# A latent-attention and ternary-GLU kernel: order of the first block's transfers, roots, transposes and queries

## The chip, the cores and the metric

The kernel runs on one core of a Trainium2 chip, in one launch. The metric is the device time of that core in microseconds (us). A core has TensorE (PE, with its weight loads PEld), VectorE (DVE), ScalarE (ACT), GpSimd (POOL) and SyncE (SP), which here does nothing but issue transfers. Each engine takes its own instructions in order. Times inside a profile are counted from the start of its span.

## The reference

The input is x, 4096 rows of 512 (two sequences of 2048). A normalised copy of x goes through an attention over 64 fixed latent keys for each of 16 heads, in which only the four largest logits of a row and head are kept; the result is normalised and added to x. Then a gated expert layer follows whose three weights are reduced to the signs -1, 0, 1 times one scale for each matrix; its result is normalised and added as well.

```python
Q = (hidden_states @ Wq.T + bq)...
V = (hidden_states @ Wv.T + bv)...
attn_logits = einsum('bhtd,lhd->bhtl', Q, latent) / sqrt(HD)
topk_logits, topk_idx = top_k(attn_logits, 4)
attn_weights = softmax(topk_logits)
weighted = einsum('bhtk,bhtkd->bhtd', attn_weights, selected)
return (weighted + V)... @ Wo.T + bo
...
scale = mean(abs(w)) + EPS                  # ternary_quant, for wu, wg and wd
q = clip(round(w / scale), -1, 1) * scale
...
hidden = silu(x @ wu.T) * (x @ wg.T)
return hidden @ wd.T
...
x = x + layernorm(attention(layernorm(x)))
x = x + layernorm(ffn(layernorm(x)))
```

The three scales need the sum of absolute values of the whole of a matrix. So no sign of a weight can be formed before that matrix has been read and summed.

## The kernel before

**Tiling.** The 4096 rows are worked in eight blocks of 512 rows, each of four tiles of 128 rows. The 2048 expert columns are 16 chunks of 128. For a block, an expert loop runs over the 16 chunks: the `u` product (8 matmuls: four slices of the 512 inputs, each with a high and a low half of the input), the `g` product likewise, the gate on ACT and DVE, and the `down` product of the chunk before it. Between these instructions stand the pieces of the next block's attention, so PE has both to do.

**The first stretch.** Block 0 has no expert loop to hide its attention. Its instructions, the reading and summing of the expert weights and the first part of block 1's attention are put in an order written out by hand, the string `FIRST_STEPS`. Each word is a step with its tile, head pair or piece: the table `STEPS` says what it calls, and nothing is reordered later. Words that the change touches:

- `ast`, `ars`, `aap`, `atr`, `acp`: block 0's first normalisation. Statistics of a tile on DVE (L245, L246), its root on POOL (`rstd`, L252 and L253), the normalised row on DVE (L272), its transposition on PE into a PSUM bank (`transpose_row`, L282) and the copy to SBUF (ACT, and DVE for tile 2; L591, L589). Before, `ars` works on two tiles at a time.
- `q`, `qc`: a query chunk on PE (L597) and its copy with the bias on ACT (L604). `bh`, `bl`: bias of the output, which reads bo. `l`, `lc`: logits of two head pairs and their copy on ACT (L622). `m`, `r`, `e`, `n`: the four largest, their replacement, the exponentials, the weights. `v`, `t`, `tc`, `y`, `yc`, `o`: values, transposed weights, their product, output.
- `su`, `sg`, `sd` with a piece number: sum of absolute values of one piece of raw weights on ACT (L202). u and g have eight pieces of 512 KB, d has six of 512 KB and four of 256 KB. `totu`, `totg`, `totd`: the sums over partitions on PE (L210). `scu`, `scg`, `scd`: the scales on DVE. `rd`: rounding on POOL (L226); signs follow on ACT (L233). `scd` also makes the scale of the output (L843 to L847).
- `nst`, `nap`, `ntr`, `ncp`, `nq`, `nqc`: the same normalisation and the four queries of block 1. `nq1`, `nq2`, `nq3` stand behind the first block's last outputs.
- `ost`, `onm`, `oap`, `oad`: the output's normalisation. `fst`, `frs`, `fap`, `ftr`, `fhi`, `flo`: the normalisation ahead of the experts. Statistics, root, row, transposition on PE, the high half on ACT (L701), the low half on DVE (L707). Then block 0's expert loop begins (L724 for `u` and `g`, L767 for `down`).

**PSUM.** There are eight banks: two for `at_psum` (used in turn by logits, transposes, block 1's queries and totals), one each for `u` and `g`, four for `acc_psum` (block 0's queries, then its four output tiles, then the expert accumulators). In a turn, a bank is taken again when its last reader is done.

**Transfers.** All go through SP's queue in the order of the program: block 0's four x tiles, wq, lk (the latent keys), bqv (biases), wv, lv, bo, block 1's x, the u pieces 0 to 7, g 0 to 7, wo, d 0 to 9. Each word of `FIRST_STEPS` that reads one of them waits for its landing. SP issues a transfer only when an earlier one, some eight before it, has landed.

**Order around the change.** At the start: x, statistics, roots, rows, transposes, copies, then the first query. At the end: block 1's queries 1, 2, 3 on PE, then the four transposes in the two banks of `at_psum`, the total of d in the same banks, and the first expert product.

Of the kernel before, what the change touches and what calls it, by code (L numbers as in the profile page):

```python
# [17 lines left out]
P = 128  # L18
# [14 lines left out]


FIRST_STEPS = """
ast0 ast1 ast2 ars0 ast3 aap0 ars1 aap1 atr0 aap3 atr1 acp0 aap2 atr3 acp1 atr2 acp3 acp2 q0 bh
q1 qc0 bl nst0 l0 nst3 qc1 su0 nst1 v0 lc0 nst2 lc1 nrs su2 m1 su3 m0 l1 su1 r0 q2 lc2 su5 nap0
e0 r1 su6 ntr0 qc2 q3 ncp0 nap3 su7 nap1 nap2 sg1 n0 sg2 ob0 ob1 m2 ob2 e1 v1 qc3 n1 lc3 sg4 r2
sg5 t0 t1 tc0 ob3 tc1 m3 ntr2 e2 ntr1 ncp2 r3 y0 ncp1 l2 yc0 sg7 o3_0 n2 e3 o2_0 sd0 n3 v3 lc5
lc4 m5 sd2 m4 sd3 t3 r4 t2 su4 o0_0 tc2 o1_0 tc3 r5 sd6 y1 sd7 l3 yc1 e4 o1_1 lc7 n4 e5 o0_1 lc6  # L40
o2_1 n5 sd9 totu sd8 t4 o3_1 tc4 scu sg6 m6 rdu2 t5 v2 tc5 r6 rdu4 sgu2 rdu6 sgu4 m7 rdu0 sgu6
ntr3 y2 ncp3 r7 sgu0 nq0 yc2 e6 e7 n6 sg0 o0_2 n7 nqc0 sd1 t6 o2_2 tc6 t7 sg3 o1_2 tc7 totg sd5
y3 scg rdg6 o3_2 yc3 rdg4 o2_3 sgg6 o3_3 ost2 rdg0 sgg4 o1_3 ost3 ors2 sgg0 o0_3 ost1 ors3 nq1
sd4 onm2 ost0 ors1 oap2 onm3 oap3 ors0 oad2 oad3 rdg2 onm0 fst2 oap0 nq2 nqc1 oad0 frs2 sgg2
onm1 fst3 oap1 fap2 frs3 oad1 fst1 nq3 nqc2 fap3 frs1 fst0 fap1 frs0 ftr3 fap0 nqc3 fhi3 ftr0
flo3 fhi0 flo0 ftr1 fhi1 ftr2 flo1 fhi2 flo2 totd scd rdd0 rdd1
"""

LAST_O = ((0, 3), (1, 3), (2, 3), (3, 3))
# [9 lines left out]
def latent_attention_ternary_glu(  # L59
# [15 lines left out]
    nc = tc.nc  # L75
    NT, D = x_in.shape
    E = wuT.shape[1]
    DC = D // P
# [18 lines left out]
    def at_psum(name):  # L97
        return ps_at.tile([P, 512], F32, tag="at", name=name)
# [11 lines left out]
    def transposed(which, b, name, dtype):  # L110
        return work.tile([P, DC, TB], dtype, tag=f"{which}{b % 2}", name=name, bufs=1)
# [8 lines left out]
    halves = [(k, h) for k in range(DC) for h in range(2)]  # L120
    raw = {}
# [5 lines left out]
    count = {"u": 2 * DC, "g": 2 * DC, "d": 2 * DC + 2}  # L127

    def load_x(b):
        x_tiles[b] = []  # L130
        for t in range(TT):
            xt = work.tile([P, D], F32, tag="x", name=f"x_{b}_{t}", bufs=2 * TT)
            r = b * TB + t * P
            nc.sync.dma_start(out=xt, in_=x_in[r : r + P, :])
            x_tiles[b].append(xt)
# [7 lines left out]
            out=normed[b], in_=x_in[b * TB : (b + 1) * TB, :].rearrange("(t p) d -> p t d", p=P)  # L143
        )

    def load_up(n, src):
        for i, (k, h) in enumerate(halves):
            nc.sync.dma_start(
                out=raw[n, i], in_=src[k * P : (k + 1) * P, h * CH : (h + 1) * CH]
            )  # L150

    load_x(0)
    wq = wpool.tile([P, DC, D], F32, name="wq")
    wv = wpool.tile([P, DC, D], F32, name="wv")
    wo = wpool.tile([P, DC, D], F32, name="wo")
    bqv_sb = wpool.tile([P, 2, DC], F32, name="bqv_sb")
    bo_sb = wpool.tile([P, D], F32, name="bo_sb")
    lk = wpool.tile([P, DC, 2 * L], F32, name="lk")
    lv = wpool.tile([P, H // 2, HP], F32, name="lv")
    nc.sync.dma_start(out=wq, in_=wqT.rearrange("(c p) n -> p c n", p=P))  # L160
    nc.sync.dma_start(out=lk, in_=latk)
    nc.sync.dma_start(out=bqv_sb, in_=bqv)
    nc.sync.dma_start(out=wv, in_=wvT.rearrange("(c p) n -> p c n", p=P))
    nc.sync.dma_start(out=lv, in_=latv)
    nc.sync.dma_start(out=bo_sb, in_=bo.to_broadcast([P, D]))
    load_x(1)
    load_up("u", wuT)
    load_up("g", wgT)
    nc.sync.dma_start(out=wo, in_=woT.rearrange("(c p) n -> p c n", p=P))
    for i in range(count["d"]):  # L170
        rows = 2 * P if i < 6 else P
        r = i * 2 * P if i < 6 else 12 * P + (i - 6) * P
        nc.sync.dma_start(
            out=raw["d", i].rearrange("p (c n) -> p c n", n=D),
            in_=wdT[r : r + rows, :].rearrange("(c p) n -> p c n", p=P),
        )


    both = work.tile([P, 2, P], F32, tag="hid", name="ones", bufs=2)
# [14 lines left out]
    tern = {}  # L194
# [5 lines left out]
    def sum_abs(n, i):  # L200
        w = raw[n, i]
        nc.scalar.activation(  # L202
            junk[:, : w.shape[-1]], w, AF.Abs, accum_out=sums[n][:, i : i + 1]
        )

    totals = {}

    def total(n):
        totals[n] = at_psum(f"tot_{n}")
        nc.tensor.matmul(  # L210
            totals[n][:, : count[n]], lhsT=ones, rhs=sums[n], start=True, stop=True
        )

    def scale(n):
        total = small.tile([P, 1], F32, tag="wtotal", name=f"total_{n}", bufs=1)
        nc.vector.tensor_reduce(total, totals[n][:, : count[n]], AX.X, ALU.add)
        sc = columns[:, 1 + "ugd".index(n) : 2 + "ugd".index(n)]
        nc.vector.tensor_scalar(sc, total, 1.0 / (D * E), QUANT_EPS, ALU.mult, ALU.add)
        scales[n] = sc
        inv = columns[:, 4 + "ugd".index(n) : 5 + "ugd".index(n)]  # L220
        nc.vector.reciprocal(inv, sc)
        inverses[n] = inv
# [53 lines left out]
    def row(name):  # L276
        return work.tile([P, D], F32, tag="row", name=name, bufs=4)

    def transpose_row(h, name):
        pt = at_psum(f"pt_{name}")  # L280
        for c in range(DC):
            nc.tensor.transpose(pt[:, c * P : (c + 1) * P], h[:, c * P : (c + 1) * P], ident)  # L282
        return pt.rearrange("p (c k) -> p c k", k=P)
# [288 lines left out]
    class FirstAttention(SecondAttention):  # L572
# [12 lines left out]

        def a_copy(self, t):
            dst, src = self.hT[:, :, t * P : (t + 1) * P], self.pt.pop(t)
            if self.b == 0 and t == 2:
                nc.vector.tensor_copy(dst, src)  # L589
            else:  # L590
                nc.scalar.copy(dst, src)  # L591

        def q_pe(self, c, psum):
            self.pq = getattr(self, "pq", {})
            self.pq[c] = psum(f"pq_{self.b}_{c}")
            for k in range(DC):
                nc.tensor.matmul(  # L597
                    self.pq[c], lhsT=wq[:, k, c * P : (c + 1) * P], rhs=self.hT[:, k, :],
                    start=(k == 0), stop=(k == DC - 1),
                )  # L600

        def q_copy(self, c, qT):
            self.qT[c] = qT
            nc.scalar.activation(qT, self.pq.pop(c), AF.Identity, bias=bqv_sb[:, 0, c : c + 1])  # L604
# [88 lines left out]
            nc.vector.tensor_tensor(x_tiles[self.b][t], x_tiles[self.b][t], self.rows.pop(("o", t)), ALU.add)  # L693

        def f_trans_pe(self, t):
            self.pt[t] = transpose_row(self.rows.pop(("f", t)), f"f{self.b}_{t}")

        def f_high(self, t):
            if not hasattr(self, "hi"):
# [13 lines left out]
    class Experts:  # L713
# [5 lines left out]

        def up(self, n, e):  # L720
            p = ps_up.tile([P, TB], F32, tag=n, name=f"p{n}_{self.b}_{e}")
            for k in range(DC):
                for i, part in enumerate(self.parts):
                    nc.tensor.matmul(  # L724
                        p, lhsT=tern[n, 2 * k + e // 8][:, (e % 8) * P : (e % 8 + 1) * P], rhs=part[:, k],
                        start=(k == 0 and i == 0), stop=(k == DC - 1 and i == 1),
                    )
            (self.pu if n == "u" else self.pg)[e] = p


# [97 lines left out]
    A = FirstAttention(0)  # L828
    nxt = FirstAttention(1)
# [6 lines left out]
        half_u.append(half)  # L836

    def scale_out():
        scale("d")

        first = columns[:, 8:9]
        square = columns[:, 9:10]
        nc.vector.tensor_scalar(first, half_u[0], scales["g"], scales["d"], ALU.mult, ALU.mult)  # L843
        nc.vector.tensor_tensor(square, first, first, ALU.mult)
        least = columns[:, 10:11]
        nc.vector.reciprocal(least, square)
        nc.vector.tensor_scalar(least, least, LN_EPS, 0.0, ALU.mult, ALU.add)  # L847
        out_scale.extend((first, square, least))


    def query_place(c):
        if c < 3:
            if not hasattr(nxt, "early"):
                nxt.early = transposed("Y", 1, "qT_1", F32)
            return nxt.early[:, c, :]
        return work.tile([P, TB], F32, tag="qT", name=f"qT_1_{c}", bufs=1)


    def first_query_place(c):
        tag = ("hid_hi", "hid_lo")[c // 2]  # L860
        return work.tile([P, TB], F32, tag=tag, name=f"qT_0_{c}", bufs=2)

    STEPS = {
        "ast": A.a_stats,
        "ars": lambda j: A.a_rstd(2 * j, 2 * j + 2),
        "aap": A.a_apply,
        "atr": A.a_trans_pe,
        "acp": A.a_copy,
# [1 line left out]
        "qc": lambda c: A.q_copy(c, first_query_place(c)),  # L870
        "l": A.l_pe,
        "lc": A.l_copy,
        "m": A.m,
        "r": A.r,
        "e": A.e,
# [24 lines left out]
        "ntr": nxt.a_trans_pe,  # L900
        "ncp": nxt.a_copy,
        "nq": lambda c: nxt.q_pe(c, at_psum),
        "nqc": lambda c: nxt.q_copy(c, query_place(c)),
        "totu": lambda: total("u"),
        "totg": lambda: total("g"),
        "totd": lambda: total("d"),
        "scu": half_scale,
        "scg": lambda: scale("g"),
        "scd": scale_out,
    }  # L910
    for n in "ugd":
        STEPS["s" + n] = lambda i, n=n: sum_abs(n, i)
        STEPS["rd" + n] = lambda i, n=n: rounded(n, i)
        STEPS["sg" + n] = lambda i, n=n: sign(n, i)
    for step in FIRST_STEPS.split():
        name, numbers = re.fullmatch(r"([a-z]+)([0-9_]*)", step).groups()
        STEPS[name](*(int(v) for v in numbers.split("_") if v))

# [143 lines left out]
    for b in range(NB):  # L1062
        if b > 0:
            A, nxt = nxt, after
# [141 lines left out]
```

## Time and profile before

| what | us |
|---|---|
| median of three runs (lowest, highest) | 1152.59 (1152.09, 1153.02) |
| the profiled execution | 1154.03 |
| its span | 1152.1 |
| PE, DVE, ACT, POOL busy in the span | 1134.6, 841.5, 402.6, 167.6 |
| first query matmul starts | 12.44 |
| last weight piece's stretch of full DMA traffic ends | about 51 |
| first expert matmul starts | 90.59 |
| mean granted TensorE clock | 0.997 |

The profile is of one execution. An engine's share is an average over the whole span; what a change in one stretch is worth has to be read in that stretch, in the timelines (start, duration, engine, source line, what was written from what, how often, and in brackets the idle time before with what ended it) and in tables of windows. A busy PE is a modelled figure: matmuls are pipelined, so the distance between the starts of two of them says more than the duration of one.

```profile
PEclk9999999999999999999999999999999999999999
DMA  9700211023111322133222222232321412102001
GB/s 346 302 0 1 73 56 55 1 68 116 65 46 37 111 91 74 54 102 101 85 80 73 74 95 98 65 91 75 108 76 55 110 65 93 62 1 74 37 1 37
```

These are lines of the page's 40 slices of 28.8 us: the clock granted (in tenths, 9 is 0.9 or more), the share of the 16 DMA engines and what they moved. The weights come in the first two slices.

### The profile page before, as it was taken

The numbers are of one execution on the slowest core, as the hardware profiler recorded it, in microseconds if no ns is written. First come the engines' busy times: TensorE is split into PE (matmuls) and PEld (weight loads), VectorE is DVE, ScalarE is ACT, GpSimd is POOL, SyncE is SP. The second block draws the span as 40 slices with busy tenths as digits, with TensorE's granted clock in tenths as the row PEclk, the third lists the DMA queues.
The fourth block names the chain that finished last, engine by engine and source line by source line (L and its number), as shares of the span: only waits on it lengthen the run. The fifth ranks groups of instructions, "written<-read, shape, count | busy, mean of one in ns | idle before, by whom it ended". The sixth has DMA issues, their size and how long they took to land.

```text
span 1152.1 us, 14493 instructions
## 1 busy us (share of the span) xinstructions
PE 1134.6 (98%) x4650; PEld 776.8 (67%) x4650; DVE 841.5 (73%) x2939; ACT 402.6 (35%) x701; POOL 167.6 (15%) x203
## 2 busy tenths in 40 slices
PE   8999999999999999999999999999999999999997
PEld 5547665876757676676657766586675766768785
DVE  6976984968866978668876788677886787847435
ACT  4985531332313332333314333143322433224223
POOL 1056001310022100320003200022001120030100
PEclk9999999999999999999999999999999999999999
DMA  9700211023111322133222222232321412102001
GB/s 346 302 0 1 73 56 55 1 68 116 65 46 37 111 91 74 54 102 101 85 80 73 74 95 98 65 91 75 108 76 55 110 65 93 62 1 74 37 1 37
DMA packets 89355, 90.87 MB, mean 79 GB/s; under 512 B 7872, under 2 KB 62400, under 8 KB 89280
## 3 DMA queue, kind: packets, MB, share of 16 engines
q1 hardware_dynamic: 89280, 89.95, 24.5%
q8 instruction: 37, 0.61, 0.2%
q14 instruction: 38, 0.31, 0.1%
HBM read 56.37 MB, written 33.55 MB: 78 GB/s over the span
## 4 chain that ended last, share of the span: by engine, by line
PE 88%; DVE 5%; DMA 3%; ACT 2%; SPq 1%; issue 0%; POOL 0%; DVEq 0%; ACTq 0%
PE pg L724 20%; PE acc L767 19%; PE pu L724 19%; PE po L464 8%; PE pv L436 8%; PE pq L349 7%; PE pv L453 2%; PE pl L363 2%; DMA raw_d<-in_wdT 1%; DMA raw_g<-in_wgT 1%; PE pq L597 1%; DMA bo_sb<-in_bo 1%; DVE left L389 1%; DMA raw_u<-in_wuT 1%; ACT junk L202 1%; PE pt_f L282 0%
## 5 line engine op out<-in xcount | busy, mean ns | idle before, releaser
L724 PE MATMUL pg<-hT_f,tern_g 128*128 128x512 f32 x512 | 208.3, 407 | 0.0
L724 PE MATMUL pu<-hT_f,tern_u 128*128 128x512 f32 x512 | 205.5, 401 | 0.0
L767 PE MATMUL acc<-tern_d,hi 128*128 128x512 f32 x512 | 203.5, 398 | 0.0
L767 PE MATMUL acc<-tern_d,lo 128*128 128x512 f32 x512 | 200.0, 391 | 2.3 <-DVE lo L757 2.1
L724 PE MATMUL pu<-lT_f,tern_u 128*128 128x512 f32 x512 | 200.4, 391 | 0.1
L724 PE MATMUL pg<-lT_f,tern_g 128*128 128x512 f32 x512 | 199.6, 390 | 0.0
L733 ACT ACTIVATE h<-pu,columns 128x512 f32<-128x512 f32 x128 | 87.1, 681 | 203.0 <-PE pu L724 202.7
L752 ACT CAST hi<-h 128x512 fp32r<-128x512 f32 x128 | 79.2, 619 | 216.8 <-DVE h L741 216.8
L736 DVE SCALAR_TENSOR_TENSOR h<-h,pu 128x512 f32<-128x512 f32 x128 | 86.0, 672 | 86.6 <-ACT h L733 86.6
L741 DVE TENSOR_TENSOR h<-h,pg 128x512 f32<-128x512 f32 x128 | 86.4, 675 | 66.4 <-PE pg L724 65.3
L767 PEld LDWEIGHTS acc<-tern_d,hi 128*128 128x128 f32 x512 | 96.1, 188 | 32.8 <-issue 13.4
L724 PEld LDWEIGHTS pg<-hT_f,tern_g 128*128 128x128 f32 x512 | 96.3, 188 | 25.4 <-issue 1.7
L767 PEld LDWEIGHTS acc<-tern_d,lo 128*128 128x128 f32 x512 | 96.1, 188 | 24.4 <-DVE lo L757 3.9
L724 PEld LDWEIGHTS pu<-hT_f,tern_u 128*128 128x128 f32 x512 | 96.5, 188 | 23.9 <-issue 2.4
L724 PEld LDWEIGHTS pu<-lT_f,tern_u 128*128 128x128 f32 x512 | 96.6, 189 | 23.0 <-issue 2.9
L724 PEld LDWEIGHTS pg<-lT_f,tern_g 128*128 128x128 f32 x512 | 96.3, 188 | 22.2 <-issue 3.4
L757 DVE TENSOR_TENSOR lo<-h,hi 128x512 fp32r<-128x512 f32 x128 | 92.5, 723 | 25.4 <-ACT hi L752 25.4
L436 PE MATMUL pv<-hT,wv 128*128 128x512 f32 x224 | 100.7, 592 | 0.2 <-ACT w L371 0.2
L389 DVE MATCH_REPLACE8 left<-m,w 128x64 f32<-128x64 f32 x512 | 100.3, 209 | 0.0
L464 PE MATMUL po<-wo,attnT 128*128 128x512 f32 x224 | 97.3, 592 | 0.0
L349 PE MATMUL pq<-hT,wq 128*128 128x512 f32 x192 | 86.6, 594 | 0.3 <-PE acc L767 0.3
L464 PEld LDWEIGHTS po<-wo,attnT 128*128 128x128 f32 x224 | 42.5, 190 | 50.8 <-issue 48.6
(144 smaller groups left out, 1317.4 us busy)
## 6 DMA issues: line engine op xcount, KB each, us to landing
dz<-z SPq DMA_DIRECT2D x56, 256.0 KB, 2.0
wT<-dz SPq DMA_DIRECT2D x224, 64.0 KB, 1.9
x<-in_x SPq DMA_DIRECT2D x32, 256.0 KB, 3.9
out_x<-x SPq DMA_DIRECT2D x31, 256.0 KB, 2.0
xa<-in_x SPq DMA_DIRECT2D x6, 1024.0 KB, 5.3
far_a<-za SPq DMA_DIRECT2D x20, 256.0 KB, 3.0
hT<-far_a SPq DMA_DIRECT2D x20, 256.0 KB, 5.3
far_f<-zf SPq DMA_DIRECT2D x20, 256.0 KB, 2.8
```

The source lines that it names most:

```text
L349: nc.tensor.matmul(pq, lhsT=wq[:, k, c * P : (c + 1) * P], rhs=self.taken(k), start=(k == 0), stop=(k == DC - 1),)
L363: nc.tensor.matmul(pls[pr][:, t * P : (t + 1) * P], lhsT=qT[rows, t * P : (t + 1) * P], rhs=lk[rows, c, :], start=True, stop=True, tile_po ...
L389: nc.vector.match_replace(left[:, g, :], m8[:, g, :], w[:, g, :], TAKEN)
L436: nc.tensor.matmul(self.pv[c], lhsT=wv[:, k, c * P : (c + 1) * P], rhs=self.ordered(k), start=(k == 0), stop=False,)
L464: nc.tensor.matmul(self.po[t], lhsT=self.attnT[:, c, t * P : (t + 1) * P], rhs=wo[:, c, :], start=(c == 0), stop=(c == DC - 1),)
L724: nc.tensor.matmul(p, lhsT=tern[n, 2 * k + e // 8][:, (e % 8) * P : (e % 8 + 1) * P], rhs=part[:, k], start=(k == 0 and i == 0), stop=(k = ...
L733: nc.scalar.activation(self.h[e], self.pu[e], AF.Tanh, scale=half_u[0])
L736: nc.vector.scalar_tensor_tensor(self.h[e], self.h[e], 1.0, self.pu.pop(e), ALU.add, ALU.mult)
L741: nc.vector.tensor_tensor(self.h[e], self.h[e], self.pg.pop(e), ALU.mult)
L752: nc.scalar.copy(hi, self.h[e])
L757: nc.vector.tensor_tensor(lo, self.h.pop(e), self.hid[e][0].bitcast(F32), ALU.subtract)
L767: nc.tensor.matmul(self.acc[t], lhsT=part[:, t * P : (t + 1) * P], rhs=wd, start=(e == 0 and i == 0), stop=(e == EC - 1 and i == 1),)
```

## The change

1. **`hold`.** A new step behind the first tile's statistics clears one column of the lk tile on DVE and then issues every transfer that stood behind wq. lk's transfer writes the same place, so it waits for that clearing, and SP's queue stands behind it.
2. **Order of transfers.** The pieces of u, g and d are issued in another order, with wo between the fourth and the fifth piece of g.
3. **Roots tile by tile.** `ars` takes a range of tiles: 0 and 1, then 2, then 3. The rows, transposes and copies run in the order 0, 1, 2, 3, and tile 3's copy is the one on DVE.
4. **Block 1's last query in parts.** `nq3` becomes four pieces of two passes each (`nqp3_0` to `nqp3_3`), put between the transposes `ftr2`, `ftr3`, `ftr1`, `ftr0`; its copy `nqc3` comes behind the high halves.
5. **Banks.** Transposes of tiles 0 and 1, the parts of the query and the total of d use `acc_psum`.
6. **Total and scale.** `totd` stands ahead of the transposes. `scd` makes the scale of d alone, before the last low halves; the scale of the output becomes its own step `sco` behind them.
7. **First expert.** In block 0's first `u` product, the four matmuls of the high half come first, then those of the low half. One further step, `sg5`, stands five words later.

```diff
-ast0 ast1 ast2 ars0 ast3 aap0 ars1 aap1 atr0 aap3 atr1 acp0 aap2 atr3 acp1 atr2 acp3 acp2 q0 bh
+ast0 hold ast1 ars0_2 ast2 ars2_3 ast3 ars3_4 aap0 aap1 atr0 aap2 atr1 acp0 aap3 atr2 acp1 atr3 acp2 acp3 q0 bh
...
-onm1 fst3 oap1 fap2 frs3 oad1 fst1 nq3 nqc2 fap3 frs1 fst0 fap1 frs0 ftr3 fap0 nqc3 fhi3 ftr0
-flo3 fhi0 flo0 ftr1 fhi1 ftr2 flo1 fhi2 flo2 totd scd rdd0 rdd1
+onm1 fst3 oap1 fap2 frs3 oad1 totd fst1 ftr2 nqc2 fhi2 nqp3_0 fap3 frs1 fst0 ftr3 nqp3_1 fhi3 fap1
+frs0 flo2 ftr1 nqp3_2 fhi1 fap0 ftr0 nqp3_3 fhi0 scd flo3 flo1 flo0 sco nqc3 rdd0 rdd1
...
+    def load_weights():
+        nc.sync.dma_start(out=lk, in_=latk)
...
+        load_x(1)
+        load_up("u", wuT, (0, 2, 3, 1, 5, 6, 7, 4))
+        load_up("g", wgT, (1, 2, 4, 5))
+        nc.sync.dma_start(out=wo, in_=woT.rearrange("(c p) n -> p c n", p=P))
+        load_up("g", wgT, (7, 6, 0, 3))
+        for i in (0, 2, 3, 6, 7, 9, 8, 1, 5, 4):
...
     def total(n):
-        totals[n] = at_psum(f"tot_{n}")
+        totals[n] = (acc_psum if n == "d" else at_psum)(f"tot_{n}")
...
-            if self.b == 0 and t == 2:
+            if self.b == 0 and t == 3:
                 nc.vector.tensor_copy(dst, src)
...
+        def q_part(self, c, k, psum):
+            if k == 0:
+                self.pq[c] = psum(f"pq_{self.b}_{c}")
+            nc.tensor.matmul(
+                self.pq[c], lhsT=wq[:, k, c * P : (c + 1) * P], rhs=self.hT[:, k, :],
+                start=(k == 0), stop=(k == DC - 1),
+            )
...
         def f_trans_pe(self, t):
-            self.pt[t] = transpose_row(self.rows.pop(("f", t)), f"f{self.b}_{t}")
+            psum = at_psum if t in (2, 3) else acc_psum
+            self.pt[t] = transpose_row(self.rows.pop(("f", t)), f"f{self.b}_{t}", psum)
...
+            pairs = [(k, i) for k in range(DC) for i in range(2)]
+            if self.b == 0 and e == 0 and n == "u":
+
+                pairs.sort(key=lambda pair: pair[1])
...
     def scale_out():
-        scale("d")
...
+    def hold_weights():
+        nc.vector.memset(lk[:, 0, 0:1], 0.0)
+        load_weights()
...
-        "ars": lambda j: A.a_rstd(2 * j, 2 * j + 2),
+        "ars": A.a_rstd,
...
+        "nqp": lambda c, k: nxt.q_part(c, k, acc_psum),
...
-        "scd": scale_out,
+        "scd": lambda: scale("d"),
+        "sco": scale_out,
```

More of the change, by code (lines that the diff above doesn't have):

```diff
@@ L35 @@
 FIRST_STEPS = """
-ast0 ast1 ast2 ars0 ast3 aap0 ars1 aap1 atr0 aap3 atr1 acp0 aap2 atr3 acp1 atr2 acp3 acp2 q0 bh
+ast0 hold ast1 ars0_2 ast2 ars2_3 ast3 ars3_4 aap0 aap1 atr0 aap2 atr1 acp0 aap3 atr2 acp1 atr3 acp2 acp3 q0 bh
 q1 qc0 bl nst0 l0 nst3 qc1 su0 nst1 v0 lc0 nst2 lc1 nrs su2 m1 su3 m0 l1 su1 r0 q2 lc2 su5 nap0
 e0 r1 su6 ntr0 qc2 q3 ncp0 nap3 su7 nap1 nap2 sg1 n0 sg2 ob0 ob1 m2 ob2 e1 v1 qc3 n1 lc3 sg4 r2
-sg5 t0 t1 tc0 ob3 tc1 m3 ntr2 e2 ntr1 ncp2 r3 y0 ncp1 l2 yc0 sg7 o3_0 n2 e3 o2_0 sd0 n3 v3 lc5
+t0 t1 tc0 ob3 tc1 sg5 m3 ntr2 e2 ntr1 ncp2 r3 y0 ncp1 l2 yc0 sg7 o3_0 n2 e3 o2_0 sd0 n3 v3 lc5
 lc4 m5 sd2 m4 sd3 t3 r4 t2 su4 o0_0 tc2 o1_0 tc3 r5 sd6 y1 sd7 l3 yc1 e4 o1_1 lc7 n4 e5 o0_1 lc6
@@ L144, in load_normed, with load_up @@
         )
-    def load_up(n, src):
-        for i, (k, h) in enumerate(halves):
+    def load_up(n, src, pieces):
+        for i in pieces:
+            k, h = halves[i]
             nc.sync.dma_start(
@@ L160, in latent_attention_ternary_glu @@
     nc.sync.dma_start(out=wq, in_=wqT.rearrange("(c p) n -> p c n", p=P))
[L161 to L176, printed above, removed]
+    def load_weights():
+        nc.sync.dma_start(out=lk, in_=latk)
+        nc.sync.dma_start(out=bqv_sb, in_=bqv)
+        nc.sync.dma_start(out=wv, in_=wvT.rearrange("(c p) n -> p c n", p=P))
+        nc.sync.dma_start(out=lv, in_=latv)
+        nc.sync.dma_start(out=bo_sb, in_=bo.to_broadcast([P, D]))
+        load_x(1)
[4 more added lines that the diff above has]
+        for i in (0, 2, 3, 6, 7, 9, 8, 1, 5, 4):
+            rows = 2 * P if i < 6 else P
+            r = i * 2 * P if i < 6 else 12 * P + (i - 6) * P
+            nc.sync.dma_start(
+                out=raw["d", i].rearrange("p (c n) -> p c n", n=D),
+                in_=wdT[r : r + rows, :].rearrange("(c p) n -> p c n", p=P),
+            )
     both = work.tile([P, 2, P], F32, tag="hid", name="ones", bufs=2)
@@ L277, in row, with transpose_row @@
         return work.tile([P, D], F32, tag="row", name=name, bufs=4)
-    def transpose_row(h, name):
-        pt = at_psum(f"pt_{name}")
+    def transpose_row(h, name, psum=at_psum):
+        pt = psum(f"pt_{name}")
         for c in range(DC):
@@ L600, in q_pe @@
                 )
+        def q_part(self, c, k, psum):
[4 more added lines that the diff above has]
+                start=(k == 0), stop=(k == DC - 1),
+            )
         def q_copy(self, c, qT):
@@ L721, in up @@
             p = ps_up.tile([P, TB], F32, tag=n, name=f"p{n}_{self.b}_{e}")
[L722 to L727, printed above, removed]
+            pairs = [(k, i) for k in range(DC) for i in range(2)]
+            if self.b == 0 and e == 0 and n == "u":
+                pairs.sort(key=lambda pair: pair[1])
+            for k, i in pairs:
+                nc.tensor.matmul(
+                    p, lhsT=tern[n, 2 * k + e // 8][:, (e % 8) * P : (e % 8 + 1) * P],
+                    rhs=self.parts[i][:, k], start=(k, i) == pairs[0], stop=(k, i) == pairs[-1],
+                )
             (self.pu if n == "u" else self.pg)[e] = p
@@ L872, in latent_attention_ternary_glu @@
         "lc": A.l_copy,
+        "hold": hold_weights,
         "m": A.m,
```

## The prediction

> **What bounds the kernel now.** I read the busy shares first, then ten- and two-microsecond windows to find where TensorE is not full, then the engines' timelines there. Times are from the span's start.
>
> ```profile
> PE 1134.6 (98%) x4650; PEld 776.8 (67%) x4650; DVE 841.5 (73%) x2939; ACT 402.6 (35%) x701; POOL 167.6 (15%) x203
> ...
> 84.00:86.00 2.00, 2.00 (x6) 0.90 (x5) 1.25 (x4) 0.00 (x0) 1.51 (x4) 1.00 0.01 4
> 86.00:88.00 2.00, 1.40 (x9) 0.78 (x7) 0.94 (x2) 1.38 (x3) 0.00 (x0) 1.00 0.00 0
> 88.00:90.00 2.00, 1.31 (x8) 0.84 (x8) 1.33 (x3) 1.11 (x3) 0.00 (x0) 1.00 0.00 0
> 90.00:92.00 2.00, 1.52 (x5) 1.10 (x6) 1.73 (x7) 0.43 (x1) 0.28 (x1) 0.85 0.00 0
> 92.00:94.00 2.00, 2.00 (x6) 1.53 (x5) 1.16 (x3) 0.00 (x0) 2.00 (x3) 0.50 0.06 12
> ```
>
> The first line is the page's; the others are windows (columns: length, PE, PEld, DVE, ACT and POOL busy, granted clock, DMA share, GB/s). TensorE bounds the whole, so a gain must be time that PE waits or runs slowly. Such time lies here in two places: the start, and 86 to 95, where PE idles and is then granted half its clock.
>
> ```profile
> 75.85 10.46 PE L597 MATMUL pq<-hT,wq 128*128 128x512 f32 x24
> 86.15 0.60 PE L282 MATMUL pt_f<-ident,h_f 128*128 128x128 f32 x4
> 87.09 0.66 PE L282 MATMUL pt_f<-ident,h_f 128*128 128x128 f32 x4 [0.34 <-ACT qT L604]
> 88.29 0.66 PE L282 MATMUL pt_f<-ident,h_f 128*128 128x128 f32 x4 [0.55 <-DVE lT_f L707]
> 89.15 0.66 PE L282 MATMUL pt_f<-ident,h_f 128*128 128x128 f32 x4 [0.20 <-DVE lT_f L707]
> 90.35 0.39 PE L210 MATMUL tot_d<-sums_d,ones 128*128 128x10 f32 x2 [0.55 <-DVE lT_f L707]
> 90.59 0.48 PE L724 MATMUL pu<-hT_f,tern_u 128*128 128x512 f32 x1
> 91.21 0.66 PE L724 MATMUL pu<-lT_f,tern_u 128*128 128x512 f32 x1
> ```
>
> PE's timeline (start, duration, idle before and releaser): the second block's last three queries, then four row transposes that wait for two PSUM banks to be emptied by ACT and DVE, then the sum for the down weights, then the experts.
>
> ```profile
> 5.68 0.69 DVE L245 BATCH_NORM_STATS2 st_a<-x 128x6 f32<-128x512 f32 x1 [0.28 <-DMA x<-in_x]
> 7.44 0.69 DVE L245 BATCH_NORM_STATS2 st_a<-x 128x6 f32<-128x512 f32 x1 [0.84 <-DMA x<-in_x]
> 9.83 1.00 DVE L272 TENSOR_SCALAR h_a<-x,mv_a,rs_a 128x512 f32<-128x512 f32 x2 [0.59 <-POOL rs_a L253]
> 12.44 7.10 PE L597 MATMUL pq<-hT,wq 128*128 128x512 f32 x16 [0.83 <-ACT ones L660]
> 22.31 1.11 DVE L381 MAX8 m<-w 128x8 f32<-128x64 f32 x8 [0.90 <-ACT w L622]
> 43.27 1.06 ACT L202 ACTIVATE junk<-raw_d 128x1024 bf16<-128x1024 f32 x1 [0.33 <-DMA raw_d<-in_wdT]
> 46.20 1.06 ACT L202 ACTIVATE junk<-raw_d 128x1024 bf16<-128x1024 f32 x1 [0.80 <-DMA raw_d<-in_wdT]
> 53.12 0.19 DVE L404 TENSOR_REDUCE ri<-top 128x8 f32<-128x32 f32 x1 [0.49 <-ACT top L398]
> ```
>
> These are lines of the DVE, PE and ACT timelines up to 70. From 12.44 three engines are nearly full together (ten-microsecond windows give DVE 88 to 96%, ACT 85 to 97% between 20 and 50), and DMA moves about 400 GB/s until 51. ACT waits for raw_d at 43.27 and 46.20, so an earlier start is worth only what the transfers let through.
>
> **Part 1, the start.** After the first tile's statistics DVE now clears one column of lk (0.1 us, as its other small memsets at 0.09), and lk's transfer, with all behind it on SP's queue, waits for that. lk was issued at 3.05; now after the statistics end (4.44), about 4.6: 1.55 later. Behind it stand bqv, wv, lv, bo, the second block's x and all expert weights. Ahead are x and wq, 2.1 MB, of which the windows up to 4.5 have moved about 0.8; at the 400 GB/s seen later the rest lasts beyond 7.7. The first x was issued at 0.72 and its bytes show between 1.5 and 2.0, so lk's would flow at about 5.9. The engines stay fed: I cost the hold at 0 for the stream, bounded by +1.55 (the whole delay) and -2.0 (2 to 8.5 us moved about 270 GB/s; at 390 the same bytes need 2.0 less).
>
> The last x tile lands at 7.4, and wq's early bytes compete with it anyway; I take 0.4 for it (0 to 1.8, if it followed the third by no more time than its statistics). Roots tile by tile take away the 0.59 wait at 9.83. So q0 starts about 1.0 earlier (0.6 to 2.4). POOL issues six small operations rather than four (0.19 and about 0.6 each), beside DVE's work.
>
> What comes through? DVE's first max (22.31) waits for ACT, but its own statistics of the second block end at 21.41, after the bias row that needs bo (15.55, same place in the stream): at most 0.85 of gain there. At 43.27 ACT sums raw_d 0. Ahead of it in the new order are the same bytes (all u and g, wo), so it still lands at 43.25, and the two logit copies behind it on ACT release DVE's next max at 44.9 instead of 45.25: only 0.35 is left. But raw_d 1 now comes after 2 and 3, each of which lands 0.5 MiB, 1.36 us, earlier (ten such transfers follow at 1.35 to 1.45). ACT then runs 43.27 + 1.1 + 1.05 (copies) + two sums of 1.18 + raw_u 4 at 1.18, ending at about 48.8 against 49.9: 1.1 earlier. DVE, 0.35 earlier, no longer waits 0.49 at 53.12 nor 0.1 behind it: 0.9 to 1.0. From there DVE and ACT hand on to each other to PE's sum at 69.97. **I take 1.0**, bounds -0.55 (1.0 less 1.55) and +2.0. wo four transfers earlier removes PE's 0.34 wait at 41.97, inside the same 1.0.
>
> **Part 2, queries between transposes.** From 75.85 PE has: 24 query matmuls, 10.30 to the next start; four rows of transposes at 0.53 each (61.05 to 61.58 elsewhere in the timeline); the sum at 0.32. Together 12.74, so the experts could begin at 88.59 instead of 90.59: **2.0**. For this every transpose must find its row and bank. With nothing else moved, PE asks for row 2 at 83.0, row 3 at 84.4, row 1 at 85.8, row 0 at 87.2 (two queries to 82.7, then the sum, and after each transpose a piece of 0.86). Rows are normalised at 81.64, 83.98, 85.24 and 86.49 by DVE's timeline: slack 1.4, 0.4, 0.6, 0.7. Banks: rows 2 and 3 use those of queries 1 and 2, whose copies end by 80.2 and 83.6; the sum, the query and rows 1 and 0 use the four output banks, the last of which is read at 81.88. The extra low half on DVE ahead of row 0 (0.69) fills the 0.71 in which DVE waits for the last root; without that cover it would cost at most 0.69, against 0.7 of slack. The last query's copy (ACT, 0.69) moves behind the high halves, before the tanh, where ACT idled 4.1. Starting 1.0 earlier moves all these together.
>
> **Part 3, order of the first expert and the scale.** With all high halves first, PE has four matmuls (0.91) while the last low half is made: high half 0.6 after the transpose, then 0.7. The piece of 0.86 and the 0.91 cover 1.3. So the wait before 91.21 goes: 0.39. DVE's scale (0.5) is before the last low halves: row 0's normalisation ends 86.49, three scale steps to 87.0, then two low halves to 88.4, and the last when its high half is there: no delay. Rounding on POOL starts about 5 earlier, like PE; the rest of the scale (1.7, of which one step took 1.02 beside POOL) ends before the first silu.
>
> **Part 4, the clock.** The first 16 expert matmuls take 90.59 to 96.35, 5.76; the next 16 take 3.65 (0.228 each). Of the 2.11 lost, 0.39 is the wait above and **1.7** the half clock, granted from 91.4 to 94.8. It follows a stretch of 4.3 with only transposes and the small sum; the window before it (84.6 to 88.0) was half queries and was not throttled. After the change every 3.4 holds over half query work, so I count all 1.7.
> [...]
>
> **Sum.** 1.0 + 2.0 + 0.39 + 1.7 = 5.1. The profiled execution took 1154.03 (span 1152.1 and 1.93 around it): 1148.9 for it. The median of the runs shown is 1.44 lower, 1152.59, so **1147.5**. Behind 96 PE is full (windows of 9.6 to 10.0 in ten), and DVE, full from 110, is fed by PE's logits, so the shift is passed on.
>
> **Rivals.**
> (a) The half clock is not gained. The profiled execution is 1.44 over the median, near the 1.7; the timed runs may not have had it. [...] Then 1152.59 - 3.4 = 1149.2.
> [...]
> (b) The held transfers make x and the stream faster, by up to 2.0: the start gives 2.0, 1146.5. For it: the low rate from 3.5 to 8.5. Against it: only wq, which isn't held, directly follows x.
> (c) The interleaving does not work: a row or bank is later than PE by more than its slack, PE waits between pieces as before, and the idle, 2.0, and the half clock stay. Then 1.0 + 0.39 remain: 1151.2, no measurable change. POOL's roots, at a rough 0.9 each, speak for it; the slack of every step against it.
> (d) Slower: the hold empties the DMA engines. SP issues nothing until DVE, behind the first x, has cleared lk; each us that the engines stand empty is added to raw_d's landing at 43 and from there to PE. From a release later than about 6.4 (7.7 less 1.3 to first bytes) the stream slips; the change is slower once the slip is over 6.1 (5.1 and the 1.0 of the order lost with it). A slip of 9 gives 1155.5. Only a first x tile several us later than 3.5 would do it.
>
> **From cases to numbers.** Forecast 0.60, (a) 0.18, (b) 0.07, (c) 0.09, (d) 0.06. What a measurement tells from no change is about 0.2%, 2.3 us: 1150.3 to 1154.9. Forecast, (a) and (b) are faster, and a share of (c): 0.87; the rest of (c) is the same, 0.07; slower 0.06. The range goes from (b) with its full bounds, 1145.6, to (a) with the start lost as well, 1150.2; the likeliest's own is 1146.5 to 1149.0.
>
> **What would show it.** q0's first matmul at about 11.4; raw_d's first sum still waiting, near 43; PE without idle from the queries to the first pu, near 87.6; clock 1.00 there; the second expert's pu near 91.2 (96.35 before). Wrong: idle between the pieces, a clock of 0.5 behind them, or raw_d landing a microsecond or more later.

## The result and the profile after

The changed kernel took 1149.34 us (median of 11, 1148.79 to 1152.65), the kernel before in the same comparison 1153.02 (11 runs). The ratio is 0.9972 (95% interval 0.9964 to 0.9979): 3.2 us faster, interval 2.4 to 4.2. Forecast were 1147.5 and a gain of 5.1. The direction was right. The time is 1.8 us above the forecast: inside the whole range (1145.6 to 1150.2), above the span that the prediction gave its likeliest case (1146.5 to 1149.0), and next to the 1149.2 of rival (a).

Two executions of the changed kernel stand apart, at 1152.55 and 1152.65. The second of them is the first profile that was taken, so this profile must be read with care. These are windows of it (length, PE, PEld, DVE, ACT, POOL busy, granted clock, DMA share, GB/s):

```profile
8.00:10.00 2.00, 0.93 (x8) 0.84 (x8) 1.89 (x6) 0.26 (x1) 1.21 (x2) 1.00 1.01 337
10.00:12.00 2.00, 1.77 (x10) 1.14 (x8) 0.46 (x1) 1.60 (x4) 0.00 (x0) 0.70 1.04 399
12.00:14.00 2.00, 1.18 (x2) 0.69 (x3) 0.69 (x1) 0.00 (x0) 0.00 (x0) 0.50 1.05 376
...
16.00:18.00 2.00, 2.00 (x4) 0.82 (x3) 1.47 (x3) 0.43 (x1) 0.00 (x0) 0.59 1.05 417
```

From about 11 to nearly 18 us the clock is halved, from the last of block 0's transposes on. The timelines of DVE and PE in the same profile say what became of the start:

```profile
7.58 0.69 DVE L249 BATCH_NORM_STATS2 st_a<-x 128x6 f32<-128x512 f32 x1 [0.98 <-DMA x<-in_x]
...
8.41 2.05 DVE L276 TENSOR_SCALAR h_a<-x,mv_a,rs_a 128x512 f32<-128x512 f32 x4
...
12.82 9.49 PE L601 MATMUL pq<-hT,wq 128*128 128x512 f32 x16 [0.83 <-ACT ones L672]
```

The fourth x tile was not early (7.58, 7.44 before). The 0.59 wait between the rows is gone: DVE makes four in a row. The 16 records of the queries then take 9.49 us where they took 7.10.

A second profile of the same kernel (first experiment below, 1149.71) has clock 1.00 there. It is the one to set against the kernel before. Its PE timeline in the place where the forecast put most of the gain:

```profile
82.06 0.29 PE L214 MATMUL tot_d<-sums_d,ones 128*128 128x10 f32 x2
82.20 0.64 PE L286 MATMUL pt_f<-ident,h_f 128*128 128x128 f32 x4
82.68 1.02 PE L609 MATMUL pq<-hT,wq 128*128 128x512 f32 x2
83.54 0.60 PE L286 MATMUL pt_f<-ident,h_f 128*128 128x128 f32 x4
83.97 1.02 PE L609 MATMUL pq<-hT,wq 128*128 128x512 f32 x2
84.83 0.60 PE L286 MATMUL pt_f<-ident,h_f 128*128 128x128 f32 x4
85.27 1.02 PE L609 MATMUL pq<-hT,wq 128*128 128x512 f32 x2
86.13 0.60 PE L286 MATMUL pt_f<-ident,h_f 128*128 128x128 f32 x4
86.57 1.02 PE L609 MATMUL pq<-hT,wq 128*128 128x512 f32 x2
87.41 1.20 PE L740 MATMUL pu<-hT_f,tern_u 128*128 128x512 f32 x4
88.44 1.07 PE L740 MATMUL pu<-lT_f,tern_u 128*128 128x512 f32 x4
```

No line has idle time in brackets. The first expert matmul is at 87.41 (87.6 forecast, 90.59 before), and the windows of the same profile show a full clock:

```profile
86.00:88.00 2.00, 2.00 (x10) 1.16 (x10) 1.97 (x5) 1.01 (x3) 1.59 (x2) 1.00 0.00 0
88.00:90.00 2.00, 2.00 (x10) 1.67 (x9) 0.92 (x5) 0.71 (x2) 2.00 (x3) 1.00 0.06 12
```

To follow a gain through the kernel I use the starts of ACT's tanh (L733 before), which waits for a finished `u` product, as landmarks: of the second expert of block 0, of the second of block 2, and of the ninth of the last block.

| profile | time | 2nd expert, block 0 | 2nd expert, block 2 | 9th expert, block 7 |
|---|---|---|---|---|
| before, first | 1154.03 | 98.85 | 372.35 | 1100.33 |
| before, second | 1153.36 | 98.51 | 371.84 | 1099.56 |
| before, third | 1153.90 | 98.53 | 372.14 | 1100.19 |
| after, first | 1152.65 | 96.20 | 370.59 | 1098.71 |
| after, second | 1149.71 | 93.67 | 367.28 | 1095.66 |

Behind the first stretch the second profile is 5.18 ahead of the first one of before. At the last landmark it is 4.67 ahead. Against the other two profiles of before it is 4.84 and 4.86 ahead at the first landmark, 3.9 and 4.5 at the last.

### The profile page after: what moved, and what is told of

Read it like the earlier page. It is cut to its first block, busy times and chain, and to the rows that moved or that the text cites. A ratio compares the mean times of both kernels' runs of the same rounds, so it can differ in the third digit from the quotient of the medians.

```text
span 1150.6 us, 14497 instructions
## 1 busy us (share of the span) xinstructions
PE 1134.1 (99%) x4650; PEld 776.1 (67%) x4650; DVE 840.3 (73%) x2940; ACT 402.2 (35%) x701; POOL 167.8 (15%) x205
## 3 DMA queue, kind: packets, MB, share of 16 engines
q1 hardware_dynamic: 89280, 89.95, 24.5%
## 4 chain that ended last, share of the span: by engine, by line
PE 93%; DVE 4%; DMA 1%; ACT 1%; issue 0%; SPq 0%; POOL 0%; DVEq 0%; ACTq 0%
PE pg L740 19%; PE pu L740 19%; PE acc L783 19%; PE po L468 8%; PE pv L440 8%; PE pq L353 7%; PE pv L457 3%; PE pl L367 2%; PE pq L601 2%; PE po L692 1%; PE pv L646 1%; DMA hT<-far_a 1%; DVE left L393 1%; DMA x<-in_x 0%; PE pt_f L286 0%; DVE lo L773 0%
```

## The experiments

Each variant's time is set against the kernel before on the same chip: medians 1152.67, 1153.01 and 1152.96 in the three groups.

**The changed kernel again** (no edit).

> The changed kernel once more, for a second profile. In its first profile (1152.65 us) the clock was 0.5 from about 11 to 16 us, while most timed runs were near 1149. Theory A (half clock early in some executions only): a profile at full clock from 9 to 16 us has q0's queries at 0.43 us a matmul, comes out near 1149, and its time at the first expert matmul is some 2.5 us earlier than the 89.95 of the first profile. Rival B (the spread is elsewhere): a time near 1149 with the same half clock at the start.

Measured: 1149.71, queries from 12.21 at clock 1.00 (the first four records take 1.96; two took 2.04 at half the clock), first expert matmul at 87.41 against 89.95: 2.54 earlier. This is what theory A said. Of this kernel's two profiles one has the half clock at the start (0.50 in the windows from 12 to 16), and it is 2.5 us later at the first expert and 2.9 later in time. What brings it is tested three runs below.

**The late parts alone.** The start is as before: nothing held, the old order of transfers, the old roots (only `sg5` keeps its new place).

```diff
-ast0 hold ast1 ars0_2 ast2 ars2_3 ast3 ars3_4 aap0 aap1 ...
+ast0 hold ast1 ast2 ars0_2 ast3 aap0 ars2_4 aap1 atr0 aap3 ...
...
+        load_up("u", wuT, range(8))
+        load_up("g", wgT, range(8))
...
+    load_weights()
...
-        nc.vector.memset(lk[:, 0, 0:1], 0.0)
-        load_weights()
+        pass
```

> The kernel before with only the late parts: the last query in pieces between the transposes, their banks, the total and scale, the first expert's order. My prediction's parts 2 to 4: 4.1 us faster, about 1148.9, first expert matmul 2.0 earlier than 90.59 and clock 1.00 from 86 to 96. Rival (the half clock moves instead of going): about 2.4 faster.

Measured: 1150.04, ratio 0.9978 (0.9969 to 0.9986): 2.5 faster, interval 1.6 to 3.6. The number is the rival's, its reason is not: the half clock has not moved, the profile shows 1.00 from 8 to 18 and from 84 to 98. The second expert's tanh is at 94.08, 4.8 ahead of the first profile of before (98.85). At the last landmark 3.8 of it is left (1096.52 against 1100.33), and the timed runs show 2.5. So the stretch gives more than forecast, and the time shows little more than half of it. The next runs look for the rest.

**The early parts alone.** The late lines of the list are as before.

```diff
-... oad1 totd fst1 ftr2 nqc2 fhi2 nqp3_0 fap3 frs1 fst0 ftr3 nqp3_1 ...
+... oad1 fst1 nq3 nqc2 fap3 frs1 fst0 fap1 frs0 ftr3 fap0 nqc3 ...
...
-        totals[n] = (acc_psum if n == "d" else at_psum)(f"tot_{n}")
+        totals[n] = at_psum(f"tot_{n}")
...
-            psum = at_psum if t in (2, 3) else acc_psum
+            psum = at_psum
...
-            if self.b == 0 and e == 0 and n == "u":
+            if False:
...
```

> The changed kernel with the late parts undone: hold, order of transfers and roots alone. My prediction's part 1: 1.0 us faster than before, about 1152. Rival from the changed kernel's first profile (third x tile's successor landed at 7.58 against 7.44, q0 at 12.82 against 12.44): no gain at all, or slower by up to 1.7 in executions with the half clock at 11 to 16 us.

Measured: 1153.42, ratio 1.0003 (0.9994 to 1.0012). The rival holds: no gain in the time. In the profile the queries begin at 10.79, 1.65 earlier than in the first profile of before, because the fourth x tile came early in this execution (DVE's statistics of it at 5.93). And yet the landmark (98.10) is only 0.75 earlier. ACT's timeline shows where the rest stopped:

```profile
43.65 1.06 ACT L206 ACTIVATE junk<-raw_d 128x1024 bf16<-128x1024 f32 x1 [1.64 <-DMA raw_d<-in_wdT]
```

The first piece of the down weights lands no earlier than before (43.27 there), and ACT, which came early, now waits 1.64 for it. This is the limit that the forecast named.

**The changed kernel with small matmuls at the start.** Twelve matmuls of ones into a spare bank, whose results are not read.

```diff
-ast0 hold ast1 ... atr1 acp0 aap3 atr2 acp1 atr3 acp2 acp3 q0 bh
+warm5 ast0 hold ast1 ... atr1 warm2 acp0 aap3 atr2 warm2 acp1 atr3 warm3 acp2 acp3 q0 bh
...
+    keep = gate_psum("keep")
...
+    def warm(n):
+        for i in range(n):
+            nc.tensor.matmul(keep[:, :P], lhsT=ones, rhs=ones, start=True, stop=True)
```

> The changed kernel with twelve more small ones matmuls, whose results are not read: five behind the first sixteen and two, two and three between block 0's transposes, so that TensorE is not quiet from 7 to 12 us. Theory A (the half clock after the quiet stretch makes the slow executions): no execution near 1152.6, all within a microsecond near 1149 or below, clock 1.00 from 9 to 16 us. Rival B: same spread as the changed kernel. Rival C (the added matmuls delay the transposes): all slower by up to 1 us.

Measured: 1149.58, ratio 0.9971 (0.9961 to 0.9982). All eight lie between 1148.69 and 1150.57: no execution near 1152.6, clock 1.00 from 9 to 16 in the profile. The median is no better than the changed kernel's. This fits theory A; with two such executions in eleven, eight without one are not proof by number alone. Four more variants of the changed kernel below have the same small matmuls. Over all five, none of 32 executions has a mean clock under 0.997, where the two slow ones of eleven have 0.996. One of the 32 still took 1152.20, with a mean clock of 0.998, so the half clock is not the only thing that makes an execution long.

**The kernel before again** (twice, no edit).

> The kernel before once more, for a second profile. Its first profile took 1154.03 us where the median is 1152.6 to 1153.0. Theory A (rival a of the prediction: the half clock from 91 to 95 us is not in every execution): near 1152.5, clock 1.00 there and the second expert's pu near 94.7. Theory B (half clock is there each time and the 1.4 us lie behind the first stretch): clock 0.5 somewhere between 88 and 96, second pu near 96.4 and the difference lies in waits behind 350 us.

> The kernel before a third time, for its profile. With the same late steps the half clock fell at 91 to 95 in three profiles (before twice, early parts alone) and in none at all in a fourth (early parts with small matmuls). [...] Theory B (always in the kernel before): clock 0.5 between 88 and 96 again, second pu near 96.2. [...]

Measured: 1153.36 and 1153.90, both with half the clock for some 3.4 us from about 90.9 on, second expert's pu at 96.0. This is a window of the third profile:

```profile
92.00:94.00 2.00, 2.00 (x6) 1.61 (x5) 0.92 (x3) 0.00 (x0) 2.00 (x3) 0.50 0.05 12
```

So all three profiles of before had the half clock, and none of them shows theory A. A variant whose late steps are those of before does (next but one).

**The kernel before with its late gaps filled.**

```diff
-... frs0 ftr3 fap0 nqc3 fhi3 ftr0 flo3 fhi0 flo0 ftr1 fhi1 ftr2 flo1 fhi2 flo2 totd ...
+... frs0 ftr3 fill2 fap0 nqc3 fhi3 ftr0 fill3 flo3 fhi0 flo0 ftr1 fill2 fhi1 ftr2 fill3 flo1 ...
...
```

> The kernel before with ten small ones matmuls (two, three, two, three) whose results are not read, in the gaps behind the four late transposes; nothing else. It measures the half clock alone: Theory B: 1.7 us faster than before. Theory A: 0 to 0.9 faster. If small matmuls do not keep the clock up, same as before or 0.3 slower.

Measured: ratio 1.0000 (0.9991 to 1.0009), median 1153.73 against 1153.01. In the profile the clock is 1.00 from 86 to 98, and the first sixteen expert matmuls take 4.17 instead of 5.76. The landmark (97.70) is 1.15 ahead of the first profile of before. The time does not show it: theory A's lower end. But this run does not measure the half clock alone. At the last landmark its profile is 0.23 behind the same profile of before (1100.56 against 1100.33); the 1.15 and more went into waits further on:

```profile
PE pq L349 <- DMA hT<-far_a: 1.6, 2, 0.8
```

(PE's waits: total, times, longest; what they are comes below.) The timed runs agree: 11 of its 12 executions have a mean clock of 0.998 or more, where 13 of the 23 of before beside them have, and at such a clock its mean span is 1151.4 against 1150.7. So the clock was kept, and about as much was lost elsewhere.

**The early parts with small matmuls at the start** (the edits of the early parts and of the small matmuls, together).

> The early parts alone (hold, order of transfers, roots) with the twelve small matmuls at the start. If the early parts gain about 0.75 in an execution at full clock (as the landmark of the first expert showed) and lose it where queries run at half clock, this is 0.7 to 1.2 us faster than the early parts alone, near 1152.2. If the early parts gain nothing at all: same as the early parts alone, 1153.4.

Measured: 1153.21, ratio 0.9998 (0.9989 to 1.0006): the early parts gain nothing that the time can show, also with the start kept busy. Its profile has the same late transposes with the same gaps as the kernel before. These are its windows:

```profile
88.00:90.00 2.00, 1.26 (x8) 0.83 (x7) 1.33 (x3) 1.17 (x2) 0.00 (x0) 1.00 0.00 0
90.00:92.00 2.00, 1.87 (x8) 1.42 (x8) 1.86 (x7) 0.00 (x0) 1.17 (x2) 1.00 0.00 0
92.00:94.00 2.00, 2.00 (x10) 1.57 (x9) 1.00 (x3) 1.72 (x2) 2.00 (x2) 1.00 0.01 4
```

PE is busy for 1.26 of 2.00, as little as before (1.31), and the clock stays at 1.00: the same quiet stretch does not always bring the half clock. Its landmark is 96.34, 2.5 ahead of the first profile of before: 0.88 of it is there at the first expert matmul (89.71), and 1.63 comes in the next sixteen, which take 4.13 instead of 5.76. At the last landmark 0.9 is left (1099.44).

**Weights read in the order of use**, on the variant with small matmuls at the start.

```diff
-        load_up("u", wuT, (0, 2, 3, 1, 5, 6, 7, 4))
+        load_up("u", wuT, (0, 2, 3, 1, 5, 6, 7))
...
-        load_up("g", wgT, (7, 6, 0, 3))
-        for i in (0, 2, 3, 6, 7, 9, 8, 1, 5, 4):
...
+        load_up("g", wgT, (7,))
...
+        load_down((0, 2, 3))
+        load_up("u", wuT, (4,))
+        load_down((6, 7, 9, 8))
+        load_up("g", wgT, (6, 0))
+        load_down((1,))
+        load_up("g", wgT, (3,))
+        load_down((5, 4))
```

> The changed kernel with the small matmuls at the start, and the expert weights read in the order in which they are summed (down pieces 0, 2, 3 ahead of up 4 and of gate 6, 0 and 3). If raw_d's first piece is what bounds an early start (it waited 1.64 us in the early parts alone), that wait goes and this is 0.3 to 1.0 us faster than the changed kernel with the small matmuls (1149.6). If DVE or PE bound it anyway: within 0.3 of it.

Measured: 1149.16, ratio 0.9963 (0.9950 to 0.9975); ACT waits for no piece of the down weights between 18 and 60. But neither does it in the profile of the small matmuls alone, so there was no such wait for the new order to remove. It has the lowest ratio of all, but its interval overlaps that of the small matmuls alone (0.9961 to 0.9982), and its landmark (93.52) is no earlier than theirs (93.23). Whether it gains is not settled.

**Without the hold**, in the new order and in the order of use, both with small matmuls at the start. The clearing of lk goes and everything is issued at once.

> The changed kernel with the small matmuls at the start and without the hold: lk and all behind it are issued at once, in the new order. If the hold does nothing for the stretch (my cost of 0 for the stream, 0.4 for x): within 0.4 us of the changed kernel with the small matmuls (1149.6), x's last tile's statistics near 7.5. If it brings x and wq early: 1 us slower. If it costs the stream: up to 1 us faster.

> Reading order by use, small matmuls at the start, no hold. If the hold gains nothing: same as the one with the hold (1149.2) within 0.4 us. If the hold is needed for an early start, which that order lets through: 0.5 to 1.0 slower.

Measured: 0.9971 (0.9960 to 0.9982) where the hold gives 0.9971, and 0.9965 (0.9952 to 0.9979) where it gives 0.9963. The hold does nothing that can be seen in the time. DVE's statistics of the fourth x tile begin between 5.93 and 7.58 in the seven profiles with it (mean 6.86) and between 6.47 and 7.75 in the seven without (mean 7.10). This answers rival (b) too: x does not come faster by more than its scatter.

**All late transposes in two banks**, on the variant with small matmuls at the start.

```diff
-            psum = at_psum if t in (2, 3) else acc_psum
+            psum = at_psum
...
-frs0 flo2 ftr1 nqp3_2 fhi1 fap0 ftr0 nqp3_3 fhi0 scd flo3 flo1 flo0 sco ...
+frs0 flo2 ftr1 nqp3_2 fhi1 fap0 flo3 ftr0 nqp3_3 fhi0 scd flo1 flo0 sco ...
```

> The changed kernel with the small matmuls at the start, all four late transposes in the two banks as before and one low half moved ahead of the last transpose; the pieces stay between. If the order with the pieces is what removes the idle time: 0 to 0.2 us slower than the changed kernel with the small matmuls (1149.6), no idle over 0.2 between the pieces. If the banks do it: 1 to 2 us slower with idle ahead of the third and fourth transpose.

Measured: 0.9970 (0.9959 to 0.9981), one wait of 0.24 ahead of the third transpose. From the second query of block 1 to the first expert it takes 12.66 (75.20 to 87.86), 0.45 more than with the banks of the change. So the order with the pieces removes nearly all the idle time; the banks are worth 0.45 in the profile and nothing that the time shows.

## Why the prediction was right, and where it was off

**Part 2 and 3 (queries between transposes, first expert): right, the size too small.** From the second query of block 1 to the first expert matmul the kernel before takes 14.74 (75.85 to 90.59), the second profile of after 12.21 (75.20 to 87.41). The other two profiles of before take 14.74 too. The gain is 2.53, forecast 2.0. The term that was mis-sized is PE's own time: a row of transposes costs 0.44 (83.54 to 83.97), not 0.53, and the total 0.14, not 0.32, when PE does not wait behind them. The wait ahead of the low halves is gone: the first sixteen expert matmuls end in 3.75 (87.41 to 91.16; 3.65 forecast). Rival (c), waits between the pieces, is refuted by the timeline above. The time confirms the order of size: the late parts alone gave 2.5.

**Part 1 (the start): the limit was right, the size near, the worth smaller.** Queries began at 12.21 (11.4 forecast), because x came no earlier; the second query of block 1 began at 75.20, 0.65 earlier than in the first profile of before and 0.4 earlier than in the other two; 1.0 was forecast. The path was the one predicted. ACT waits 0.50 for raw_d's first piece (43.73), is 0.64 earlier behind its sums (raw_u 4 ends at 49.25 against 49.89 before), and DVE's wait of 0.49 at 53.12 is gone. (The prediction's own sum for ACT, 43.27 + 1.1 + 1.05 + two times 1.18 + 1.18, makes 48.96 and not 48.8, so 0.9 and not 1.1.) But the time of the early parts alone shows none of it (1.0003 and 0.9998, each about 0.0009 either way). The hold's cost of 0 for the stream was right and rival (d) with it refuted: lk was issued at 4.50, 1.45 later, and raw_d's first piece came at most 0.5 later; in the profiles of the changed kernel with small matmuls, with the hold and without, it was there when ACT came to it at 43.09. The 0.4 that I gave the hold for x is not there.

**Part 4 and the sum: the step that failed.** The direction is right: in all eight profiles with queries between the transposes the clock is 1.00 from 84 to 98, where the three of before have 0.50 for some 3.4 us. What brings the half clock is not shown: that it stays away where every 3.4 holds over half query work was my estimate, from the one stretch of 84.6 to 88.0 in the first profile of before, with queries to 86.15 and a clock of 1.00. The size is not, because the prediction counted "all 1.7" of the half clock and then subtracted the whole 1.44 by which the profiled execution lay above the median. Both are partly the same thing.

Each recorded execution has a mean granted clock, rounded to a thousandth. One half-clock stretch as in the profile (half of 3.4 in 1152) takes off 0.0015. Every one of the fourteen profiles also ends with half the clock, behind the last matmul, for 2.6 to 5.7 us, which takes off 0.0011 to 0.0025 while PE has nothing left to do. So an execution should have 0.998 or 0.999 without the stretch and 0.997 or less with it, and all fourteen profiles fall on the right side of this line. (It is not sharp in every execution: one of the changed kernel with small matmuls has 0.997 and is the fastest of its eight.) In the three groups 39 of 59 executions of before have 0.998 or 0.999 and a mean span of 1150.6; 20 have 0.997 or less and 1152.0. By this sign the median execution of before does not have the half clock, and 1.7 cannot be gained on it. A third of the timed executions of before have it, and the forecast counted on it in the median one. Of the changed kernel nine of eleven have 0.998 or 0.999 and a mean span of 1147.3. Between these groups lie 3.3 us.

This is rival (a), which left 3.4 and 1149.2 without the clock and had a chance of 0.18. That it comes so near is partly luck: the late parts gave 0.53 more than it counted, the start 0.35 to 0.6 less, and the waits of the next paragraph took some as well. That the low clocks of the timed runs fall at 91 to 95 is inferred from the profiles, not seen in each; three of them have 0.994, more than one such stretch can take. And three profiles of three had the half clock where a third of the timed runs have it, which chance alone would give about one time in 25. Whether a profiled execution differs from the others in this is not known.

**What else took from it.** The prediction said that behind 96 the shift is passed on. Up to the second expert of block 1 it is: from the first landmark to there all fourteen profiles take 129.6 to 129.9. From then on it is not quite. The changed kernel and all variants but one arrive at the last landmark with 0.5 to 1.6 less of a lead over the first profile of before than they had at the first landmark; of the other two profiles of before one gains 0.4 and one loses 0.2. The waits of PE behind 340 us name the place. Of before's three profiles one has a wait there for the read-back of the transposed rows, of 0.3; the early parts with small matmuls and the first profile of after have these:

```profile
PE pq L359 <- DMA hT<-far_a: 1.7, 3, 0.9
```

```profile
PE pq L353 <- DMA hT<-far_a: 1.0, 1, 1.0
```

(total, times, longest). Over all fourteen profiles the loss goes with this wait: from the first landmark to the last it takes 1001.1 to 1002.0 us in the five that wait at most 0.3, 1002.3 to 1002.5 in the seven that wait 0.4 to 1.3, and 1002.9 and 1003.1 in the two that wait 1.6 and 1.7. In the pair that I compared it is the landing that is late, not the issue: in the first profile of before PE begins the first query behind such a read-back 7.67 after its issue (359.09 to 366.76) and does not wait for it, in the filled variant 8.26 after it (358.02 to 366.28) with a wait of 0.84. The variant with the order of use has no such wait and loses nothing (5.33 ahead at the first landmark, 5.67 at the last). The order is not the reason: the same order without the hold waits 1.0 and loses 1.0. Why the read-back lands late in most of the variants, and whether in more of their executions than of before's, stays open: only three profiles of before stand against it.

**The clock.** Behind the four late transposes of the kernel before, with gaps of at most 0.55 us between them, the clock was halved (0.50 for some 3.4 us) in four profiles of these steps and stayed at 1.00 in a fifth (the early parts with small matmuls at the start); with small matmuls or queries in the gaps it was 1.00 in every profile that has them, one and eight. Whether the transposes or the gaps bring the half clock, and why the fifth profile has none of it, no run shows.

## What to carry to other kernels

A profile is one execution: before a term that comes and goes (here the half clock behind a quiet stretch) is counted, ask whether the timed runs have it, and don't subtract the distance to the median a second time. Gaps between transposes filled with work that PE has to do anyway gained 2.5 here; filled with matmuls that nobody needs they gained nothing that the time shows. A start brought forward by 1.65 was 0.75 at the first experts, because a transfer that is needed later (raw_d) came no earlier. And a lead that a profile shows early in the kernel can be spent later: follow it to the end before it is called a gain.

## What the runs showed of the hardware that I had not expected

The start, too, had the half clock once: in the first profile of after the queries ran at 0.59 us a matmul record (9.49 for 16) instead of 0.44 (7.10 for 16), at a clock of 0.50 from 12 to 16, and that execution came out 2.9 above the second one. The three profiles of before, whose start is as quiet (PE busy for 1.07 of 2.00 from 8 to 10 in the first, 0.93 in the first of after), had the full clock there: 1.00 from 8 to 18 in the first and the third, and 2.38 for the first five query records in the second, where two took 2.04 at half the clock. So had the six profiles with small matmuls in that place (1.95 or 1.96 for the first four query records in five of them, 2.81 for the first six in the other). And holding back some 16 MB of transfers for 1.28 and 1.45 us (lk issued at 4.33 and 4.50 in the two profiles of after, at 3.05 before) moved the x tiles by no more than their scatter (5.93 to 7.58 with the hold, 6.47 to 7.75 without) and the time not at all (0.9971 with and without).
